# Four network layers on one core: one PSUM pool, Newton steps for the group norm, exponentials put off, and a helper queue with three turns and timed waits

## The chip, the cores and the metric

The kernel runs on one core of a Trainium2 chip. A core has TensorE (matrix products, PE in the profile; its weight loads are PEld), VectorE (DVE), ScalarE (ACT), GpSimd (POOL) and SyncE (SP), and DMA queues. Each engine takes its instructions in the order in which the program gives them, and waits for others by semaphores. PSUM, into which TensorE writes, has eight banks of 128 partitions x 512 fp32 values. The metric is the time of one execution on the device, in microseconds; lower is better.

## The reference, cut to what matters

All values are fp32. Four layers follow each other on `x` of shape (2, 512, 32, 32), which is 2 images of 512 channels by 1024 pixels.

```python
# layer 0: attention with a position bias from a small MLP (unchanged code), then
h1 = gelu(einsum('bchw,oc->bohw', bn(x), mlp_w1) + mlp_b1)          # 512 -> 2048
x  = x + einsum('bchw,oc->bohw', h1, mlp_w2) + mlp_b2               # 2048 -> 512
# layer 1: group norm (32 groups), 8 heads of 64, projection
g  = (g - mean) * rsqrt(var + EPS)
w  = softmax(einsum('bct,bcs->bts', q * s, k * s), axis=-1)         # per head
x  = x + proj(einsum('bts,bcs->bct', w, v))
# layer 2: group norm, one head over all 512 channels
attn = softmax(einsum('bci,bcj->bij', q, k) * C ** -0.5, axis=-1)
x  = x + proj(einsum('bcj,bij->bci', v, attn))
# layer 3: q and k of 64 channels, softmax over the FIRST index
attn = softmax(einsum('bdi,bdj->bij', q, k), axis=1)
x  = gamma * einsum('bci,bij->bcj', v, attn) + x
```

## The kernel before

**Stages.** In the profiled execution layer 0's attention runs to 2043 us and its MLP to 2450. Layer 1 follows: image 0 to about 2645, image 1 to about 2871, the projection of image 0 between. Layer 2 runs for both images to about 3160, layer 3 for both to the end. The program keeps on each engine the order in which it is written. Nothing is reordered, so what is written ahead of an instruction on its engine runs ahead of it.

**A product in seven parts.** Nearly all large products after layer 0 are made by `group`, a scheme that splits both operands in 2x2 blocks and needs seven block products in place of eight. It takes four PSUM banks x, y, v, z and gives TensorE the products in this order: x (the first), y (number 5), v (4), z (3), then more onto x (1), y (6) and v (2). ACT copies x to `p1` after the first product, and v to `p5` after the third (L1408, L1414). DVE makes `u2 = y + p1` (L1411) before product 6 may go onto y, and `u3 = y + p1` (L1420) after it; four outputs are written by `put` (L1434). Products 1 and 6 write over banks that the copy and u2 read first, so TensorE waits if those are late. `nk` is the number of 128-row steps, `n` the columns; the matmul is at L1391. One fp32 matmul instruction leaves two records in the trace.

**Forms.** The scheme needs sums of blocks of each operand: `left_sums` (DVE, L1357 to L1360; tiles `vs` for values) and `right_sums` (L1366 to L1369; tiles `pt` for weights `p`, `ot` for attention outputs), four operations for each small block, called forms below.

**The helper queue.** DVE, ACT and SP work that belongs to later groups is put as items (cost, function) into `tracks`. Each group gives it two turns: `do_chores(slack)` after `p5`, and again after the outputs. A turn runs items track by track until the costs have used up the budget. An `APART` in a track ends that track's turn, which is how a wait for a DMA is spaced. `flush` runs everything that is left in a track, at once, when the next step needs it.

**Softmax sums.** In layers 2 and 3 `Weights` holds the four chunks of p of a half (512 pixels). `acc` adds them on DVE (L1805). `total` sums over partitions with two matmuls against ones into bank `den` (L1819), copies the row and sends it to `few`, 128 partitions wide, by SP DMAs. `divisor` adds the two halves of `few`, inverts and sends the result through DRAM (`d`, L1832) to all partitions (`r`, L1833). In layer 3 (`shares=True`) each chunk of p is multiplied by r (`normalize`, L1837) and formed again before the product `pw3`; in layer 2 the product's output is multiplied (L1872). Attention of layer 1 does alike in `divide`, once per pair of heads and image: `sums`, `invert` (with the DMAs `d`, `r`), `scale` (L1636). Products are named: `pm` heads and projections, `pmv` values, `ppr` layer 1's projection, `score`, `pw` weighted values (`pw2`, `pw3` by layer).

**Group norm.** `group_norm` is a generator whose pieces are items of the queue: BN_STATS for each 128 channels, two small matmuls over groups, then, for the inverse root, `Ln` and `Exp(-0.5 ...)` on ACT and one correction step on DVE (L1103 to L1108).

**Pools.** The MLP has its own PSUM pool with three turning buffers for each of two tiles, and `ps_m` has two banks for the norm. Both close after the MLP; then `banks`, eight turning banks with one tag, opens for all the rest.

Of the kernel before, what the change touches and what calls it, by code (L numbers as in the profile page):

```python
# [19 lines left out]
P = 128  # L20
# [60 lines left out]
def kernel(ctx: ExitStack, tc: tile.TileContext, a: dict, out: bass.AP):  # L81
# [971 lines left out]
    def layers(f, fold_d, t2_b, o2_b):  # L1053
# [19 lines left out]
        def group_norm(x, gname, bname, h, small_psum):  # L1073

            st = small.tile([P, CC, 2, 6], F32, name="st")
            mv = small.tile([P, CC, 2], F32, name="mv")
            for cc in range(CC):
                for half in range(2):
                    nc.vector.bn_stats(st[:, cc, half, :], x[:, cc, half * HALF : (half + 1) * HALF])
                nc.vector.bn_aggr(mv[:, cc, :], st[:, cc].rearrange("p h s -> p (h s)"))  # L1080
                yield

            def over_group(v, name):
                pg = small_psum("pg")[:, :CC]
                nc.tensor.matmul(pg, cs("gmean"), v, start=True, stop=True)
                yield
                g = small.tile([P, CC], F32, name=name)
                nc.vector.tensor_copy(g, pg)  # L1088
                return g

            mean = small.tile([P, CC], F32, name="mean")
            nc.vector.tensor_copy(mean, mv[:, :, 0])
            yield
            gm = yield from over_group(mean, "gm")
            nc.vector.tensor_sub(mean, mean, gm)
            nc.vector.tensor_mul(mean, mean, mean)
            nc.vector.tensor_add(mean, mean, mv[:, :, 1])
            yield
            var = yield from over_group(mean, "var")
            nc.vector.tensor_scalar(var, var, EPS, None, ALU.add)  # L1100

            rs = small.tile([P, CC], F32, name="rs")
            nc.scalar.activation(rs, var, AF.Ln)  # L1103
            nc.scalar.activation(rs, rs, AF.Exp, scale=-0.5)
            nc.vector.tensor_mul(var, var, rs)
            nc.vector.tensor_mul(var, var, rs)
            nc.vector.tensor_scalar(var, var, -0.5, 1.5, ALU.mult, ALU.add)
            nc.vector.tensor_mul(rs, rs, var)  # L1108
            sc = small.tile([P, CC], F32, name="sc")
            sh = small.tile([P, CC], F32, name="sh")  # L1110
            nc.vector.tensor_mul(sc, rs, col(gname, 0, CC))
            nc.vector.tensor_mul(sh, gm, sc)
            nc.vector.tensor_sub(sh, col(bname, 0, CC), sh)
            yield
            normed = chan.tile([P, CC, HW], F32, name="hc")
            h.append(normed)
            for cc in range(CC):
                nc.scalar.activation(
                    normed[:, cc, :], x[:, cc, :], AF.Identity, scale=sc[:, cc : cc + 1], bias=sh[:, cc : cc + 1]
                )  # L1120
                yield

        norm_psum = f.enter_context(ExitStack())
        ps_m = norm_psum.enter_context(tc.tile_pool(name="ps_m", bufs=2, space=PSUM))

        h1s, h2s = [[], []], [[], []]
        norm = group_norm(
            xs[0], "gn_w", "gn_b", h1s[0], lambda name: ps_m.tile([P, HALF], F32, name=name, tag="mm")
        )
# [3 lines left out]
        with ExitStack() as mlp:  # L1133
# [8 lines left out]
            ps = mlp.enter_context(tc.tile_pool(name="mlp_ps", bufs=3, space=PSUM))  # L1142
# [43 lines left out]
            def products(left, right, cols, some, pms=None):  # L1186

                if pms is None:
                    pms = [ps.tile([P, 4, PX], F32, name=f"pm{i}") for i in "ab"]
                a, b = pms  # L1190
                at = {1: a[:, 0], 2: a[:, 1], 6: a[:, 2], 3: a[:, 3], 4: b[:, 0], 5: b[:, 1], 7: b[:, 2]}
                for i in some:
                    product(at[i], i, left, right, cols)
                return pms
# [50 lines left out]
            for c in range(MC):  # L1245
                for m in (MC + c, c):
                    pm = ps.tile([P, BLK], F32, name="pmp", tag="pma")
                    accumulate(pm, [(w1[:, k, m * P : (m + 1) * P], xn[:, k, :]) for k in range(CC)])
                    nc.scalar.activation(hid[:, m, :], pm, AF.Gelu, bias=col("mlp_b1", m))
                form1(nc.vector, slice(c * P, (c + 1) * P))  # L1250
            right1 = normed_rights(1)
            for m in (2, 3, 0, 1):
                pm = ps.tile([P, BLK], F32, name="pmp2", tag="pmb")
                accumulate(pm, [(w2[:, k, m * P : (m + 1) * P], hid[:, k, :]) for k in range(HID // P)])
                added(0, m, pm)
                if m >= 2:
                    form2(nc.vector, slice((m - 2) * P, (m - 1) * P))
# [52 lines left out]
        norm_psum.close()  # L1310
# [3 lines left out]
        banks = f.enter_context(tc.tile_pool(name="banks", bufs=8, space=PSUM))  # L1314

        def bank(name):
            return banks.tile([P, HALF], F32, name=name, tag="bank")

# [9 lines left out]
        tracks = []  # L1328
        APART = None

        def track():
            t = deque()
            tracks.append(t)
            return t

        def do_chores(budget):
            for t in tracks:
                while t and budget > 0:
                    item = t.popleft()
                    if item is APART:  # L1340
                        break
                    cost, f = item
                    f()
                    budget -= cost

        def flush(*some):
            for t in some:
                while t:
                    item = t.popleft()
                    if item is not APART:  # L1350
# [34 lines left out]
        def group(name, nk, n, stationary, moving, evict, slack, plain=False):  # L1385

            x, y, v, z = [bank(name)[:, :n] for _ in range(4)]
# [12 lines left out]
            if plain:  # L1400
# [4 lines left out]
                return  # L1405
            add(x, 0, 0)
# [8 lines left out]
            do_chores(slack)  # L1415
            add(z, 3, 3)
            add(x, 1, 1, False)
            add(y, 6, 6, False)
# [4 lines left out]
            do_chores(slack)  # L1423
# [29 lines left out]
        def statistics(steps, wait):  # L1453
            t = track()
            for i in range(CC + 5):
                t.append((1.5 if i < CC else 0.5, lambda: advance(steps)))
                if i >= CC:
                    t.extend([APART] * wait)
            return t

        def normed(t, steps, h, name):

            for _ in range(CC):
                t.extend(((0.1, lambda: advance(steps)), APART))
# [23 lines left out]
        def project(name, seven_w, seven_h, c, outs, bias, plain=False):  # L1488
# [3 lines left out]
            def evict(c11, c12, c21, c22):  # L1492
# [7 lines left out]
                rows(seven_w, slice(c * P, (c + 1) * P)), lambda i, k: seven_h[i][:, k, :], evict, 4.5, plain,  # L1500
            )

        def values(seven_w, seven_h, s, vt):
# [3 lines left out]
            def evict(c11, c12, c21, c22):  # L1507
# [7 lines left out]
                lambda i, k: seven_h[i][:, k, s * P : (s + 1) * P], lambda i, k: seven_w[i][:, k, :], evict, 2.0,  # L1515
# [34 lines left out]
        def attend(qs, ks, vt):  # L1550

            outs, late, acc = [], None, None
            for i in range(17):
                m, sp = divmod(i, 4)
                ps = {}
                if i < 16:
                    for s in (2 * sp, 2 * sp + 1):
# [9 lines left out]
                        do_chores(0.9)  # L1567
                if late is not None:
# [14 lines left out]
                    if lsp == 3:  # L1583
# [3 lines left out]
                        dividing = divide(o, acc, 3 if i < 16 else 1)  # L1587
# [13 lines left out]
        def divide(o, acc, wait):  # L1601
# [36 lines left out]
            t.extend((APART, (0.1, sums), *[APART] * wait, (0.4, invert), *[APART] * wait, (1.2, scale)))  # L1638
# [18 lines left out]
        def add_projection(x, seven_w, seven_o):  # L1657

            for c in range(2):

                def evict(c11, c12, c21, c22):
# [8 lines left out]
                    "ppr", 2, HALF, rows(seven_w, slice(c * P, (c + 1) * P)), lambda i, k: seven_o[i](k), evict, 2.0  # L1670
# [7 lines left out]
        to_v.extend((APART, APART))  # L1678
# [6 lines left out]
        to_h = statistics(norm, 2)  # L1685
# [48 lines left out]
        to_h = statistics(norm, 2)  # L1734
# [35 lines left out]
        def layer_values(seven_w, seven_h):  # L1770

            vt, unformed, sv, t_s = [], [], [], track()
# [19 lines left out]
        class Weights:  # L1792

            def __init__(self, score, order, at, shares):
                self.score, self.order, self.at, self.shares = score, order, at, shares
                self.p, self.spare, self.track = [], None, track()

            def grow(self, c):
                p = self.score(c)
                self.p.append(p)  # L1800
                if c == 1:
                    self.acc = unit("acc")
                if c:
                    first = self.p[0] if c == 1 else self.acc
                    self.track.append((1.2, lambda: nc.vector.tensor_add(self.acc, first, p)))  # L1805
                if not self.shares:
                    if c == 1:
                        self.form(0)
                    if c:
                        self.form(c)  # L1810
# [3 lines left out]
            def total(self):  # L1814
                acc = self.acc.rearrange(self.order, k=2, q=2)
                den, row = bank("den"), temp("row", HALF)
                self.few = small.tile([P, 2, HALF // P], F32, name="few2")
                for k in range(2):
                    nc.tensor.matmul(den[32 * k : 32 * k + 32], ones[:, :32], acc[:, k], start=True, stop=True)  # L1819
                nc.scalar.copy(row[:64], den[:64])  # L1820
                for k in range(2):
                    nc.sync.dma_start(
                        out=self.few[:, k], in_=row[32 * k : 32 * k + 1].rearrange("o (q n) -> o q n", q=P)
                    )

            def divisor(self):
                few = self.few[:, 0]
                nc.vector.tensor_add(few, few, self.few[:, 1])
# [22 lines left out]
            def finish(self):  # L1851
                self.track.extend((APART, (0.1, self.total), APART, APART, (0.4, self.divisor)))
                if self.shares:
                    self.track.append(APART)
# [4 lines left out]
        def weighed(name, x, qb, seven_sv, w, bias, done=None):  # L1859

            n = slice(qb * HALF, (qb + 1) * HALF)
            for g in range(2):
# [18 lines left out]
                group(name, 4, QUARTER, lambda i, s: seven_sv(i, s)[:, g * P : (g + 1) * P], w.seven, evict, 4.2)  # L1881
                yield

        def scores2(qb, seven_ts, seven_h):

            def score(c):
                p = unit("p2")

                def evict(c11, c12, c21, c22):
# [5 lines left out]
                    nc.scalar.activation(p[:, QUARTER:], p[:, QUARTER:], AF.Exp, scale=C ** -0.5)  # L1895
# [3 lines left out]
                    lambda i, k: seven_ts(i, k, qb), evict, 2.0,  # L1899
# [5 lines left out]
        for b in range(B):  # L1905
# [11 lines left out]
            if b == 0:  # L1917
# [3 lines left out]
                to_h = statistics(norm, 1)  # L1921
# [97 lines left out]
        to_x.append(APART)  # L2019
# [142 lines left out]
```

## Time and profile before

| what | value |
|---|---|
| median of 3 runs (lowest to highest) | 3422.63 us (3417.33 to 3426.73) |
| profiled execution: time, span | 3421.59 us, 3419.8 us |
| mean granted TensorE clock | 0.994 |
| TensorE busy, share of the span | 3364.8 us, 98% |
| DVE, ACT, POOL busy | 78%, 53%, 14% |
| ACT_TABLE_LOAD in the four group norms | 8 x 1.28 us (L1103, L1104) |
| `r<-d` DMAs, issue to landing (median) | 24 of them, 3.5 us |
| last matmul ends, span ends | 3413 us, 3419.8 us |

Each timeline or wait line has engine, source line, operation, and tiles as output<-inputs. A bracket at the end gives the engine's idle time before the instruction and what ended it. `x6` means that six like records are drawn together, so a line's time holds all of them. In the table of stages the columns are busy us and count for each engine, then the granted clock (1.00 is full speed), the busy share of the DMA engines and GB/s.

### The profile page before, as it was taken

The numbers are of one execution on the slowest core, as the hardware profiler recorded it, in microseconds if no ns is written. First come the engines' busy times: TensorE is split into PE (matmuls) and PEld (weight loads), VectorE is DVE, ScalarE is ACT, GpSimd is POOL, SyncE is SP. The second block draws the span as 40 slices with busy tenths as digits, with TensorE's granted clock in tenths as the row PEclk, the third lists the DMA queues.
The fourth block names the chain that finished last, engine by engine and source line by source line (L and its number), as shares of the span: only waits on it lengthen the run. The fifth ranks groups of instructions, "written<-read, shape, count | busy, mean of one in ns | idle before, by whom it ended". The sixth has DMA issues, their size and how long they took to land.

```text
span 3419.8 us, 61213 instructions
## 1 busy us (share of the span) xinstructions
PE 3364.8 (98%) x24837; PEld 1621.9 (47%) x24837; DVE 2660.2 (78%) x3421; ACT 1817.5 (53%) x2781; POOL 463.9 (14%) x563
## 2 busy tenths in 40 slices
PE   9999999999999999999999999999999999999997
PEld 4333333333333333333333339999753534678776
DVE  6999999999997999999999954555456375646555
ACT  4866867867865767867767631112136163212220
POOL 0222222222221222222222210000000000000000
PEclk9999999999999999999999999999999999999998
DMA  5676676666665576676776740000101010000010
GB/s 168 148 151 138 139 155 142 146 145 139 148 145 110 121 152 142 144 148 139 150 149 134 148 134 24 14 14 11 47 0 32 7 35 20 4 4 19 13 38 29
DMA packets 145555, 320.30 MB, mean 94 GB/s; under 512 B 29936, under 2 KB 75632, under 8 KB 144496
## 3 DMA queue, kind: packets, MB, share of 16 engines
q0 software_dynamic: 56880, 199.79, 30.7%
q1 hardware_dynamic: 87088, 111.78, 10.7%
q8 instruction: 198, 3.24, 0.4%
q10 hardware_dynamic: 1296, 4.72, 0.4%
q14 instruction: 93, 0.76, 0.1%
HBM read 71.46 MB, written 10.83 MB: 24 GB/s over the span
## 4 chain that ended last, share of the span: by engine, by line
PE 74%; DVE 18%; issue 5%; ACT 2%; DMA 1%; SPq 0%; POOL 0%; DVEq 0%; ACTq 0%; POOLq 0%
PE z L543 33%; DVE wa L526 7%; PE pw L1391 5%; PE pma L136 5%; DVE h L557 5%; PE pmb L136 4%; PE pmv L1391 3%; PE score L1564 3%; PE pv L1576 3%; PE score L1391 3%; DVE h L526 2%; PE pm L1391 2%; PE pmp L136 2%; PE pp L629 1%; PE ppr L1391 1%
## 5 line engine op out<-in xcount | busy, mean ns | idle before, releaser
L543 PE MATMUL z<-wa,cpb_w 128*32 128x512 f32 x11904 | 1779.1, 593 | 6.7 <-DVE simbias L490 3.4
L552 ACT ACTIVATE h<-z,b2h 128x1024 f32<-128x1024 f32 x1024 | 1134.8, 1114 | 529.0 <-PE z L543 505.6
L543 PE MATMUL z<-h,cpb_w 128*32 128x512 f32 x4480 | 986.3, 593 | 3.3 <-ACT h L552 2.2
L543 PEld LDWEIGHTS z<-wa,cpb_w 128*32 128x32 f32 x11904 | 493.0, 110 | 883.7 <-issue 804.8
L526 DVE CUSTOM_DVE_ANT_1 wa<-tab,tab 128x1024 f32<-128x1024 f32 x744 | 881.3, 1224 | 33.9 <-PE z L543 33.8
L557 DVE SCALAR_TENSOR_TENSOR h<-h,turn,h 128x1024 f32<-128x1024 f32 x512 | 657.1, 1283 | 8.8 <-ACT h L552 8.5
L543 PEld LDWEIGHTS z<-h,cpb_w 128*32 128x32 f32 x4480 | 256.3, 110 | 335.0 <-issue 291.7
L832 POOL DMA_DIRECT2D h<-h x255 | 226.9, 890 | 1064.3 <-DVE h L557 712.9
L526 DVE CUSTOM_DVE_ANT_1 h<-tab,tab 128x1024 f32<-128x1024 f32 x280 | 334.3, 1224 | 10.5 <-PE z L543 10.4
L1213 ACT COPY p<-pma 128x128 f32<-128x128 f32 x70 | 18.6, 265 | 301.4 <-PE pma L136 301.4
L1565 ACT ACTIVATE p<-score 128x512 f32<-128x512 f32 x256 | 130.0, 624 | 74.9 <-PE score L1564 73.9
L1205 DVE TENSOR_TENSOR upper<-pma,p 128x256 f32<-128x256 f32 x70 | 29.6, 422 | 163.4 <-ACT p L1213 163.3
L825 POOL DMA_DIRECT2D h<-h x126 | 109.8, 872 | 331.3 <-DMA h<-h 327.9
L829 POOL DMA_DIRECT2D h<-h x126 | 120.0, 952 | 137.2 <-DMA h<-h 131.9
L1597 DVE TENSOR_TENSOR acc<-acc,p 128x1024 f32<-128x1024 f32 x96 | 110.9, 1219 | 17.7 <-ACT p L1565 17.7
L1564 PE MATMUL score<-q,k 64*128 64x512 f32 x512 | 120.2, 603 | 1.1 <-DVE gm L1088 1.1
L1576 PE MATMUL pv<-p,vT 128*64 128x512 f32 x512 | 116.5, 598 | 0.0
L1391 PE MATMUL pw<-p,vT 128*128 128x256 f32 x384 | 92.4, 389 | 10.3 <-DVE p L1837 10.2
L513 ACT ACTIVATE tab<-tab,pc 128x512 f32<-128x512 f32 x126 | 96.2, 763 | 0.0
L1391 PE MATMUL pmv<-wa,hc 128*128 128x256 f32 x384 | 90.9, 384 | 2.9 <-DVE u L1420 2.1
L1391 PEld LDWEIGHTS pw<-p,vT 128*128 128x128 f32 x384 | 72.8, 193 | 27.7 <-DVE p L1837 13.6
L347 ACT ACTIVATE products<-qpad,pc 128x64 f32<-128x64 f32 x252 | 85.5, 407 | 0.0
(437 smaller groups left out, 3708.0 us busy)
## 6 DMA issues: line engine op xcount, KB each, us to landing
h<-h POOLq DMA_DIRECT2D x255, 512.0 KB, 4.9
h<-h POOLq DMA_DIRECT2D x252, 256.0 KB, 4.9
tab<-slog_d SPq DMA_DIRECT2D x128, 256.0 KB, 4.5
h<-h SPq DMA_DIRECT2D x126, 256.0 KB, 2.3
r<-d SPq DMA_DIRECT2D x24, 256.0 KB, 3.5
xt<-in_xt SPq DMA_DIRECT2D x8, 512.0 KB, 7.9
wa<-in_mlp_w SPq DMA_DIRECT2D x4, 1024.0 KB, 8.0
wb<-in_mlp_w SPq DMA_DIRECT2D x16, 256.0 KB, 5.7
```

The lines of the kernel that those rows point to most:

```text
L136: nc.tensor.matmul(pm, w, m, start=(k == 0), stop=(k == len(pairs) - 1))
L526: nc.vector._custom_dve(TENSOR_ADD_SAT, out=h1.rearrange("p (y x) -> p y x", x=W), in0=tx[:, quad, point, :].unsqueeze(1).to_broadcast([P, ...
L543: nc.tensor.matmul(z[point * 32 : point * 32 + 32, n], cpb_w2[:, lo : lo + 32], h1s[point][:, n], start=True, stop=True,)
L552: nc.scalar.activation(h2, z, AF.Relu, bias=b2h[:, part : part + 1])
L557: nc.vector.scalar_tensor_tensor(h2, h2, turn[:, part // 2 : part // 2 + 1], parts.pop(part + 1), ALU.mult, ALU.add)
L829: nc.gpsimd.dma_start(out=joins[i - 3][1:P:2], in_=joins.pop(i - 2)[1:P:2], accum_op=ALU.add)
L832: nc.gpsimd.dma_start(out=joins[i - 1], in_=other, accum_op=ALU.add)
L1391: nc.tensor.matmul(out, stationary(l, k), moving(r, k), start=start and k == 0, stop=k == nk - 1, skip_group_check=not start,)
L1564: nc.tensor.matmul(sc, ks[m][r, s * P : (s + 1) * P], qs[m][r, n], start=True, stop=True)
L1565: nc.scalar.activation(p[:, part], sc, AF.Exp, scale=64 ** -0.5)
L1576: nc.tensor.matmul(pv[half][part * 64 : part * 64 + 64], vt[s % 4][:, lo : lo + 64], lps[s, half][:, part, :], start=(s == 0), stop=(s == 7),)
L1597: nc.vector.tensor_add(acc[half], acc[half], ps[s, half])
```

## The change

- **One pool.** `ps_m` and the MLP's pool are gone. `banks` (eight banks) opens ahead of the first norm and serves the MLP's tiles too.
- **Inverse root.** `Ln`, `Exp` and the correction become an integer first guess from the bits of the variance and four Newton steps, thirteen DVE operations on 128x4 values.
- **Queue.** A track holds plain numbers as waits, in us by the queue's own clock. Each turn advances that clock by a nominal time (`nk*n/256` in a group, 3.4 in attention), and a track is passed over until its wait is up. Each group has three turns: after `p5`, after products 3 and 1, and at the end. Budgets are smaller (4.5, 4.2 and 2.0 become 2.6, 2.6 and 1.1). Waits are set at each place in place of APART. The track of the value sums of layers 2 and 3 goes first.
- **Put off.** Layer 2's exponential over 768 columns runs in the next group, after its `p5` copy; so does what belongs to the fourth chunk of p (forms, sum, hops).
- **Weights.** In layer 3 two sums, p0+p1 and p2+p3, replace the running one (two DVE additions in place of three). `total` then has four matmuls and four DMAs to `few`, and `divisor` three additions of 128x4.

```diff
-            nc.scalar.activation(rs, var, AF.Ln)
-            nc.scalar.activation(rs, rs, AF.Exp, scale=-0.5)
-            nc.vector.tensor_mul(var, var, rs)
-            nc.vector.tensor_mul(var, var, rs)
-            nc.vector.tensor_scalar(var, var, -0.5, 1.5, ALU.mult, ALU.add)
-            nc.vector.tensor_mul(rs, rs, var)
+            square = small.tile([P, CC], F32, name="square")
+            nc.vector.tensor_scalar(
+                rs.bitcast(mybir.dt.int32), var.bitcast(mybir.dt.int32), -0.5, float(0x5F3759DF), ALU.mult, ALU.add
+            )
+            for _ in range(4):
+                nc.vector.tensor_mul(square, rs, rs)
+                nc.vector.scalar_tensor_tensor(square, square, -0.5, var, ALU.mult, ALU.mult)
+                nc.vector.scalar_tensor_tensor(rs, square, 1.5, rs, ALU.add, ALU.mult)
...
-        norm_psum = f.enter_context(ExitStack())
-        ps_m = norm_psum.enter_context(tc.tile_pool(name="ps_m", bufs=2, space=PSUM))
+        banks = f.enter_context(tc.tile_pool(name="banks", bufs=8, space=PSUM))
...
-            ps = mlp.enter_context(tc.tile_pool(name="mlp_ps", bufs=3, space=PSUM))
...
-                    pms = [ps.tile([P, 4, PX], F32, name=f"pm{i}") for i in "ab"]
+                    pms = [bank(f"pm{i}").rearrange("p (j n) -> p j n", j=4) for i in "ab"]
...
+        def do_chores(us, budget):
+            clock[0] += us
             for t in tracks:
-                while t and budget > 0:
+                while t and budget > 0 and t.ready <= clock[0]:
                     item = t.popleft()
-                    if item is APART:
-                        break
-                    cost, f = item
-                    f()
-                    budget -= cost
+                    if isinstance(item, float):
+                        t.ready = clock[0] + item
+                    else:
+                        cost, f = item
+                        f()
+                        budget -= cost
...
         def group(name, nk, n, stationary, moving, evict, slack, plain=False):
+            third = nk * n / 256
...
             nc.scalar.copy(p5, v)
-            do_chores(slack)
+            at_once(later)
+            do_chores(third, slack)
             add(z, 3, 3)
             add(x, 1, 1, False)
+            do_chores(third, slack)
             add(y, 6, 6, False)
...
             evict((x, None), (v, u2), (z, u3), (p5, u3))
-            do_chores(slack)
+            do_chores(third, slack)
...
-                        do_chores(0.9)
+                        do_chores(3.4, 0.9)
...
-            t.extend((APART, (0.1, sums), *[APART] * wait, (0.4, invert), *[APART] * wait, (1.2, scale)))
+            t.extend((2.0, (0.1, sums), 5.0, (0.4, invert), 6.5, (1.2, scale)))
...
-            vt, unformed, sv, t_s = [], [], [], track()
+            vt, unformed, sv, t_s = [], [], [], track(True)
...
-                if c == 1:
-                    self.acc = unit("acc")
-                if c:
-                    first = self.p[0] if c == 1 else self.acc
-                    self.track.append((1.2, lambda: nc.vector.tensor_add(self.acc, first, p)))
...
+                if self.shares:
+                    self.grown(c)
+                else:
+                    if c:
+                        self.grown(c - 1)
+                    if c == 3:
+                        put_off.append(lambda: self.grown(3))
...
+                if c % 2 and self.shares or c == 1:
+                    self.acc.append(unit("acc"))
+                    self.add(self.acc[-1], p[c - 1], p[c])
+                elif c > 1 and not self.shares:
+                    self.add(self.acc[0], self.acc[0], p[c])
...
-                self.track.extend((APART, (0.1, self.total), APART, APART, (0.4, self.divisor)))
+                self.track.extend((2.0, (0.1, self.total), 4.0, (0.4, self.divisor)))
                 if self.shares:
-                    self.track.append(APART)
+                    self.track.append(5.0)
...
-                    nc.scalar.activation(p[:, QUARTER:], p[:, QUARTER:], AF.Exp, scale=C ** -0.5)
+                    put_off.append(
+                        lambda: nc.scalar.activation(p[:, QUARTER:], p[:, QUARTER:], AF.Exp, scale=C ** -0.5)
+                    )
```

## The prediction

> **What bounds the kernel now.** I read the page first: busy times, then the slices.
>
> ```profile
> span 3419.8 us, 61213 instructions
> PE 3364.8 (98%) x24837; PEld 1621.9 (47%) x24837; DVE 2660.2 (78%) x3421; ACT 1817.5 (53%) x2781; POOL 463.9 (14%) x563
> ...
> PEclk9999999999999999999999999999999999999998
> ```
>
> TensorE computes for 98% of the span, and the change alters no product of it but four small den matmuls. So only what TensorE does not compute, or computes slowly, can be won. The stages say where that is; the change begins at the MLP, at 2043 us.
>
> ```profile
> core 0: us, PE busy (x) PEld busy (x) DVE busy (x) ACT busy (x) POOL busy (x), PEclk, DMA share, GB/s
> 2043.00:2450.00 407.00, 407.00 (x3394) 399.43 (x3395) 203.61 (x625) 81.52 (x207) 17.80 (x31) 1.00 0.09 29
> 2450.00:2645.00 195.00, 192.97 (x762) 85.33 (x763) 112.70 (x150) 91.14 (x172) 0.00 (x0) 0.99 0.04 11
> ...
> 3160.00:3420.00 260.00, 236.41 (x1018) 180.16 (x1018) 143.30 (x292) 47.88 (x104) 0.00 (x0) 0.95 0.10 27
> ```
>
> The MLP has no idle TensorE time, so three turning PSUM buffers more or fewer win nothing there. The last stage has the most, at clock 0.95. The waits of TensorE after 2000 us name the sites:
>
> ```profile
> engine line waited for: us in total, times, longest us
> PE pw L1391 <- DVE p L1837: 10.2, 5, 3.2
> PE pw L1391 <- DVE vs L1358: 5.6, 7, 1.0
> PE score L1391 <- ACT p L1408: 2.9, 1, 2.9
> PE pmv L1391 <- DVE u L1420: 2.1, 1, 2.1
> PE pm L1391 <- issue: 2.0, 1, 2.0
> ```
>
> All of these are DVE or ACT work that stands ahead of what TensorE needs, save the last. A wait costs more than itself: matmuls behind a long one run slow. From TensorE's timeline:
>
> ```profile
> 2452.47 4.51 PE L1391 MATMUL pm<-hc,wa 128*128 128x512 f32 x6 [2.03 <-issue]
> 2966.02 3.78 PE L1391 MATMUL score<-t,hc 128*128 128x256 f32 x8 [2.90 <-ACT p L1408]
> 3351.08 4.10 PE L1391 MATMUL pw<-pt,vs 128*128 128x256 f32 x10 [0.96 <-DVE vs L1358]
> ```
>
> Elsewhere a record of 512 columns takes 0.43 us and one of 256 columns 0.2145. The first line's six should take 2.6 and took 4.5: the gap of 2.03 cost 3.9 in all. The second line's gap of 2.90 cost 6.2 with what follows it. I measured every late start of a matmul this way (start to start, less the pitch). After 2449 us they sum to 45 us; that is all that can be won.
>
> **Part by part.** Each term is this execution's stall and what I leave of it after walking the new order of DVE, ACT and the chores past it.
>
> *One pool.* The stall at 2452 is a pool that opens only when the old ones are free: TensorE waits for no data (its releaser is "issue"), while the last combined adds of the MLP end at 2453.0. With eight turning banks, the first group takes banks released long before; the forms it reads are done at 2460, five microseconds before their use. -3.9 (none stays; at worst 1.0, were the first bank one of the last add's).
>
> *Newton steps.* Two table loads stand in the chain of the norm that lies among layer 2's scores:
>
> ```profile
> 2956.70 1.28 ACT L1103 ACT_TABLE_LOAD   x1
> 2957.99 0.21 ACT L1103 ACTIVATE rs<-var 128x4 f32<-128x4 f32 x1
> 2958.22 1.28 ACT L1104 ACT_TABLE_LOAD   x1
> ...
> 2959.75 0.16 DVE L1105 TENSOR_TENSOR var<-var,rs 128x4 f32<-128x4 f32 x1 [3.55 <-ACT rs L1104]
> ```
>
> DVE stands still 3.55 us. Thirteen small operations replace four, nine more at a pitch of 0.2: +1.8, so DVE runs 1.75 earlier. The put-off exponential then clears ACT: the 768-column one took 0.84 ahead of the copy of p1 that TensorE waited for, and itself waited for DVE's sums. Without both, the copy is in time, and u2 (done 2966.7, now 2964.9) meets a need at 2964.0 to 2964.9: 0 to 1.0 stays, I take 0.6. -5.6. The other three norms lie in attention or projections where DVE's idle time cost TensorE nothing, so their six loads (7.7 us of ACT) and 5.4 us of added DVE are worth zero.
> The Trainium skill speaks here ("ScalarE: Activation LUTs", What ACT_TABLE_LOAD costs): a load of 1283 ns, and a drain of some 1380 ns besides. The row has the first figure, but the Ln starts 10 ns after its load; by the page two drains, 2.8 us, would be won on top, by the row none.
>
> *Queue: three turns, sums of values first, smaller budgets.* Forms of 0.42 (0.34 to 0.46 apart), sums of 0.69 and pixels' adds of 1.22 move among turns.
> - 2686 and 2945: u2 behind eight flushed sums, or two BN_STATS (1.28): with fewer ahead, -0.8 and -1.0. At 2907 one more 0.68 lands ahead: +0.65.
> - 3006 and 3155, each 1.4: last value sums, flushed just ahead of pw. One fewer: 0.95 stays, -0.9 for both. At 3253 den's 1.05 us of matmuls covered the sums and is moved away: 0.39 becomes 0.95, +0.55.
> - 3346 to 3352: sixteen sums flushed after the last values, 5.9 by four waits. Put first in the queue, twelve go beside the values: 0.95 stays, -4.95.
> - 3307: den waits 0.67 for a chain of three acc; two independent pairs, timed 2.0 later: -0.65.
>
> *Normalising in layer 3.* Block of one normalise (1.22) and four forms: 2.85 us on DVE, pw3 needs all four.
> - 3286: three were flushed; the 4.0 goes if the three turns of value and score groups take them, which their hops allow. -4.0 (at worst 0).
> - 3227: DVE now blocks 4.62 us on r, with u3 behind. In the new order the den and its four row transfers (two more on SP, 0.58 each) start in layer 2's last pw2 groups. r lands about 3212.7, 7 us ahead, so DVE no longer blocks; but the first normalise and its forms come in front of u2 of the first pmv, 2.2 to 3.2 us, with 1.7 of slow clock: 4.9 against 4.0. +0.9 (from -4 to +2).
> - 3378 to 3388: four blocks, no TensorE work between, 13.1. One block fits the second group of the pw3 before, three stay flushed: 3 x 2.85 + 1.7 = 10.3. -2.8 (from 0, were none to fit, to -8.5, were all).
>
> Both leftovers carry a slow clock of 1.7, from the row at 2452. The Trainium skill ("TensorE: Matmul & The Clock Gate", Part 1) puts the clock at half only after an idle window of about 3.4 us; here gaps of 2.03 had it, and 0.96 (the 3351 line) had not. By the page these two terms would be 3.4 smaller, by the rows not.
>
> *What is hidden.* Put-off grown(3) and the two-add acc: 1.2 us of DVE less per layer-3 block, where DVE is 55% busy. In attention a scale now comes two turns of 3.4 after its invert. Its r takes 9.2 (2669.8 to 2679.0 in the trace), so DVE waits about 2.4 with its acc adds behind. Already now DVE waits 14.7 us in five such places (up to 3.7), and TensorE not once. Zero; the second rival prices it.
>
> Sum: -3.9 -5.6 -0.8 -1.0 +0.65 -0.9 +0.55 -4.95 -0.65 -4.0 +0.9 -2.8 = -22.5. The profiled execution took 3421.6; 3399 by it. The median of the runs is 1.0 higher: 3400.
>
> **Rivals.** *Half of it comes back* (3412): smaller budgets leave more for the flushes, and DVE, a little behind at each, meets u2 late. For it: DVE's blocks of 2.85 us can only stand before something. Against: it is 55 to 61% busy there. Price: 3286 and 3378 stay (+6.8) and 3227 takes its bad end (+1.1), some 4 late u2 of 1 us each: +12.
>
> *Slower* (3433): in attention DVE's wait for r counts. Eight divides x 2.4 = 19 us of late acc and bank copies, each with 1.7 of slow clock, 14: 33 on 3400. It decides once DVE falls over about 8 us behind, the lag that acc bears now without a wait of TensorE. The five free waits in the trace speak against it.
>
> *Nearly all goes* (3385): 3378 by 8.5 rather than 2.8, 3227 by 4.0 rather than +0.9, 2907 and 3253 stay where they are, and the three leftovers of 0.95 go: 5.7 + 4.9 + 1.2 + 2.9 = 15 more.
>
> **How the numbers follow.** My forecast (3393 to 3407) 0.55, half back 0.22, nearly all 0.13, slower 0.10. The range 3384 to 3416 leaves out the slower case and the far tail of half back. 0.3% is 10.3 us, about what a measurement of this kernel can tell from no change: faster lies below 3412.4. Forecast and nearly all are there whole, 0.68; half back for some half, 0.11. Same takes the rest of half back and a little of the slower case, 0.13; slower 0.08.
>
> **What would show it.** Right: no gap at the first pm after the MLP; no ACT_TABLE_LOAD at L1103; the score wait on L1408 gone; vs waits below 3.5 us in total; the p L1837 wait still there, last and longest, some 6 to 8 us. Wrong: a wait of TensorE for acc or o in attention; more than 3 us on u lines among the pmv of layer 3; a span above 3410.

## The result, and the profile after

| | before | changed |
|---|---|---|
| median of 5 runs (lowest to highest) | 3425.15 us (3417.33 to 3426.73) | 3404.29 us (3400.25 to 3404.69) |
| ratio, 95% interval | | 0.9941 (0.9927 to 0.9956) |
| profiled execution: time, span | 3421.59, 3419.8 us | 3400.25, 3398.4 us |
| mean granted clock | 0.994 | 0.997 |

The changed kernel is faster by 0.59%: 20 us, between 15 and 25. The forecast was 3400 within 3384 to 3416. First the same parts of the page, after:

```profile
span 3398.4 us, 61331 instructions
PE 3351.9 (99%) x24853; PEld 1615.5 (48%) x24853; DVE 2662.6 (78%) x3461; ACT 1803.4 (53%) x2764; POOL 464.0 (14%) x563
```

TensorE does the same products and, in four blocks of layer 3, two den matmuls more (8 matmuls, 16 records; the prediction named only four), and yet it is busy for 13 us less. Busy time includes slow matmuls, so part of the gain is speed and not waiting. The waits of TensorE after 2400 us (line waited for: us in total, times, longest):

```profile
PE pw L1392 <- DVE p L1853: 6.9, 3, 3.1
PE pmv L1392 <- DVE u L1413: 5.2, 3, 3.7
PE pw L1392 <- DVE vs L1357: 3.5, 4, 0.9
PE score L1568 <- DVE gm L1088: 1.1, 1, 1.1
PE score L1392 <- DVE u L1413: 0.7, 1, 0.7
```

"Issue" and the score's wait on L1408 (now L1410) are gone, vs went from 5.6 to 3.5, p from 10.2 to 6.9. Before, the waits after 2400 us that the view lists came to 26.6 us; these are 17.4. That is 9.2 of 21. The late starts measured as in the prediction (start to start, less the pitch) went from 44.9 to 24.4 us, 20.5 less, so the other 11 us are matmuls that no longer run slow behind a wait, and starts too little late for the view. (Both sums hold 1.3 us at a score that waits for `gm`, the same in both kernels, which the table leaves out.)

By site, in us, each from its own trace (a0 and a1 are the program's names for the first and second half of image 0 in layer 3, and a block is the normalise and the four forms of one chunk of p):

| site in before's trace | before | forecast left | changed |
|---|---|---|---|
| 2452, first pm after the MLP | 3.9 | 0 | 0 |
| 2686 and 2945, u2 | 1.8 | 0 | 0 |
| 2907, u2 of pmv | 0.9 | 1.55 | 1.8 (1.43 and a new 0.41) |
| 2966, score | 6.2 | 0.6 | 0.85 |
| 3006, 3155, 3253, vs | 3.2 | 2.85 | 3.1 |
| 3227, first pmv of layer 3 | 4.0 | 4.9 | 5.6 |
| 3286 and 3307, a1's blocks, den | 4.7 | 0 | 0 |
| 3346, vs of the last half | 5.9 | 0.95 | 1.04 |
| 3378, last normalise blocks | 13.1 | 10.3 | 10.6 |

The gap after the MLP is closed, and the score's wait is now one of u2. From TensorE's timeline:

```profile
2448.23 1.95 PE L136 MATMUL pma<-hid,w2s 128*128 128x128 f32 x16
2450.01 8.32 PE L1392 MATMUL pm<-hc,wa 128*128 128x512 f32 x19
...
2965.73 1.13 PE L1392 MATMUL score<-t,hc 128*128 128x256 f32 x4 [0.68 <-DVE u L1413]
```

Nineteen records of 0.43 are 8.2 us: no gap and full speed.

### The profile page after: what moved, and what is told of

Same layout as the page of the kernel before. It is cut to its first block, busy times and chain, and to the rows that moved or that the text cites. A ratio compares the mean times of both kernels' runs of the same rounds, so it can differ in the third digit from the quotient of the medians.

```text
span 3398.4 us, 61331 instructions
## 1 busy us (share of the span) xinstructions
PE 3351.9 (99%) x24853; PEld 1615.5 (48%) x24853; DVE 2662.6 (78%) x3461; ACT 1803.4 (53%) x2764; POOL 464.0 (14%) x563
## 4 chain that ended last, share of the span: by engine, by line
PE 77%; DVE 16%; issue 4%; ACT 2%; DMA 1%; ACTq 0%; POOL 0%; DVEq 0%; SPq 0%; POOLq 0%
PE z L543 35%; DVE wa L526 6%; PE pma L136 5%; PE pw L1392 5%; PE pmb L136 4%; DVE h L557 4%; PE pmv L1392 4%; PE score L1568 3%; PE pv L1580 3%; PE pm L1392 3%; PE score L1392 3%; DVE h L526 2%; PE pmp L136 2%; PE pp L629 2%; PE ppr L1392 1%
## 5 line engine op out<-in xcount | busy, mean ns | idle before, releaser
L526 DVE CUSTOM_DVE_ANT_1 h<-tab,tab 128x1024 f32<-128x1024 f32 x280 | 332.9, 1216 | 10.5 <-PE z L543 10.4
```

The source lines that it names most:

```text
L526: nc.vector._custom_dve(TENSOR_ADD_SAT, out=h1.rearrange("p (y x) -> p y x", x=W), in0=tx[:, quad, point, :].unsqueeze(1).to_broadcast([P, ...
```

## The experiments

Ratios are to runs of the kernel before on the same chip; numbers at a site come from the run's one profiled execution, and the span is that execution's. The changed kernel's ratio is 0.9941.

**One part alone, on the kernel before.**

```diff
-        norm_psum = f.enter_context(ExitStack())
-        ps_m = norm_psum.enter_context(tc.tile_pool(name="ps_m", bufs=2, space=PSUM))
+        banks = f.enter_context(tc.tile_pool(name="banks", bufs=8, space=PSUM))
...
-            ps = mlp.enter_context(tc.tile_pool(name="mlp_ps", bufs=3, space=PSUM))
```

> The kernel before with the one pool of eight banks alone. Theory (each stall is a cost by itself, and goes with the edit that lies at its site): the late start of the first pm after the MLP, 3.9 us with its slow clock, goes and every other wait stays; 3.9 us less, 3419. Rival (parts lean on each other): with the first heads 4 us earlier the forms of layer 1 or its statistics come late instead, a new wait on vs or u lines before 2560 us, and the time stays within 1 us.

0.9996 (0.9987 to 1.0005). The first pm's late start is gone, but the time did not follow clearly: a slow stretch that cost 3.4 us came at 2655 us, behind products that nothing in the edit touches (see the last section). No late vs or forms of layer 1: the rival's wait did not come.

```diff
-            nc.scalar.activation(rs, var, AF.Ln)
-            nc.scalar.activation(rs, rs, AF.Exp, scale=-0.5)
...
+            for _ in range(4):
+                nc.vector.tensor_mul(square, rs, rs)
...
```

> The kernel before with the Newton steps alone. Theory: DVE's 3.55 us of idle time in layer 2's scores becomes 1.8 us of work, so the score wait on L1408 (2.90 us, 6.2 with slow clock) shrinks by 1.75 to about 1.15, which is too short for a slow clock: 4 to 5 us less, and the other three norms give nothing. Rival (the exponential ahead of the copy is the cause): the wait stays over 2 us and the gain is under 2 us.

0.9996 (0.9987 to 1.0005), but at its site the theory held. The wait on the copy fell from 2.9 us, with no slow clock behind it:

```profile
PE score L1393 <- ACT p L1410: 1.1, 1, 1.1
```

The late start went from 6.2 to 1.3, 4.9 less; the other three norms gave nothing. The time does not show it clearly: its interval runs from 4.4 us less to 1.7 more.

```diff
-                    nc.scalar.activation(p[:, QUARTER:], p[:, QUARTER:], AF.Exp, scale=C ** -0.5)
+                    put_off.append(lambda: nc.scalar.activation(p[:, QUARTER:], p[:, QUARTER:], AF.Exp, scale=C ** -0.5))
```

> The kernel before with the put-off alone: layer 2's 768-column exponential and what belongs to the fourth chunk, in its old queue of two turns. Theory: the copy of p1 is no longer behind the exponential, but DVE still idles 3.55 us for the two table loads, so u2 comes at about 2966.7 against a need at 2964: the wait on L1408 turns into a wait on the u line of some 2.3 us with a slow clock behind; 1 to 2.5 us less. Rival (the exponential is the cause): the whole wait goes, 5.6 us less.

1.0002 (0.9993 to 1.0011). As expected the wait changed its name: u2 in place of the copy, 3.1 us. The late start fell to 3.3, as no slow clock followed in this profile, but the time did not fall by the 1 to 2.5 us expected. The wait did not go, so the exponential was no cause by itself.

Both of these edits together:

> The kernel before with Newton steps and put-off, no other part. Theory: the stall at 2966 falls from 6.2 to under 1.0, as in the changed kernel, 5.2 to 5.6 us less, 3416 to 3417; the stalls of layer 3 stay as before. Rival (the queue's three turns are needed for it): more than 2 us stay.

0.9991 (0.9982 to 1.0). 0.73 and 0.17 are left of 6.2: 5.3 less at the site, without the third turn. So at the site Newton does 4.9 of it, put-off the small rest, and alone put-off moves the wait. The time is some 3 us less, with an interval that reaches no change.

**One part undone, in the changed kernel.**

```diff
-            vt, unformed, sv, t_s = [], [], [], track(True)
+            vt, unformed, sv, t_s = [], [], [], track()
```

> The changed kernel, but the track of the value sums of layers 2 and 3 stands in its old place instead of first. Theory: the first of the sixteen vs operations of layer 3's last half are left for the flush again, and the four waits of about 1 us at the start of its pw3 come back for 1.0: 4 to 5 us more than the changed kernel, about 15 us less than before. Rival (the third turn alone gives them room): under 1.5 us more.

0.9930 (0.9918 to 0.9942): not slower at all. The first theory fell; the rival's bound (under 1.5 us more) holds, but not its reason. The vs waits did come back, 5.1 us in place of 3.5 (3.7 of late starts at the last half), but the last normalise blocks, 10.6 us, vanished:

```profile
PE pmv L1392 <- DVE u L1413: 5.7, 3, 3.5
PE pw L1392 <- DVE vs L1357: 5.1, 6, 1.0
PE score L1568 <- DVE gm L1088: 1.1, 1, 1.1
PE score L1392 <- DVE u L1413: 0.7, 1, 0.7
```

There is no line for p. The sums of values, put first, use up the budgets of the turns, and the last half's acc waits behind them. In the changed kernel acc of p2 and p3 ran at 3334.8; its divisor and first normalise were these:

```profile
3346.64 0.18 DVE L1845 RECIPROCAL few<-few 128x4 f32<-128x4 f32 x1
...
3352.66 1.23 DVE L1853 TENSOR_TENSOR p<-p,r 128x1024 f32<-128x1024 f32 x1 [4.51 <-DMA r<-d]
```

With the sums last, acc ran at 3324.3, and DVE did not wait for r:

```profile
3334.21 0.18 DVE L1845 RECIPROCAL few<-few 128x4 f32<-128x4 f32 x1
...
3341.77 1.22 DVE L1853 TENSOR_TENSOR p<-p,r 128x1024 f32<-128x1024 f32 x1
```

What the prediction took for room in the turns is the time at which r lands. The reverse was tried too, the sums first in the kernel before, with nothing else:

> The kernel before, with the track of the value sums put first and nothing else changed. Theory (each stall is its own): the four vs waits of layer 3's last half shrink to one, 4.5 to 5 us less than before. Rival (sums put first delay the last half's acc, and with it r and the normalise blocks): the stall of the last flush, 13.1 in before, already has all four blocks behind it and grows by the time that r is later, 2 to 4 us; the net gain is under 2.5 us.

1.0042 (1.0029 to 1.0056), 14 us slower. The rival named the mechanism, and priced it too low:

```profile
PE pw L1391 <- DVE p L1837: 25.4, 8, 9.5
...
3388.72 0.18 DVE L1829 RECIPROCAL few<-few 128x4 f32<-128x4 f32 x1
3394.89 1.23 DVE L1837 TENSOR_TENSOR p<-p,r 128x1024 f32<-128x1024 f32 x1 [5.73 <-DMA r<-d]
```

The wait on normalise grew from 10.2 to 25.4. The vs waits of the last half fell as they should (5.9 to 1.75 of late starts), but the divisor came after the last outputs, and DVE stood 5.7 us for r with all four blocks behind it (late starts 13.1 to 19.4); a1's blocks went the same way (4.0 to 16.4). In the changed kernel, then, the other parts of the queue must first make up for this.

```diff
-            third = nk * n / 256
+            half = nk * n / 256 * 1.5
...
             add(x, 1, 1, False)
-            do_chores(third, slack)
             add(y, 6, 6, False)
...
```

> The changed kernel with two turns in each group and the old budgets (4.5, 4.2, 2.0), the clock of the queue advanced by half a group at each; waits in us, sums first, put-off, Newton and pool stay. Theory: what is won by the order and the hops stays (first pm, score, vs), but larger turns put more ahead of u2, and the normalise blocks crowd: late u lines grow by 1 to 2 us each at some three places and the stall at a1's normalise (4 us before) comes back in part; 3 to 8 us more than the changed kernel. Rival (turns do not matter, only order and waits): within 2 us of the changed kernel.

0.9950 (0.9938 to 0.9962), about 3 us more, with intervals that overlap, and 4.4 in the span, of which 3.3 is the slow stretch at 2655 us again. So the total does not tell the two expectations apart. At the sites it is a trade: a1's blocks are flushed again (9.7 us of late starts, where the changed kernel has none) and one u2 is 2.2 late, but the last blocks come to 2.4 in place of 10.6 and the first pmv to 0.4 in place of 5.6.

```diff
-                if c % 2 and self.shares or c == 1:
+                if c == 1:
...
-                elif c > 1 and not self.shares:
+                elif c > 1:
```

> The changed kernel with one running sum in layer 3 again: three additions of 1.22 in place of two, and den with two matmuls and two DMAs in place of four. Theory: 1.2 us of DVE more in each of four blocks, and den 1 us later behind the third addition: 0 to 3 us more, most of it in the normalise blocks of the last half (one fewer fits ahead of the flush would be 2.9 more). Rival (four row DMAs at 0.58 each are what makes r late, DVE blocked 5.2 us on it at 3197): the block shortens by over 1 us, and the time falls by 1 to 3 us.

0.9963 (0.9950 to 0.9977), some 7 us more, 5.1 in the span, which is over what either expected. Late starts of 5.5 at a1's blocks come back. The rival has a part of the truth too, in the first pmv: 2.3 in place of 5.6. Its divisor stands one turn later there, and its first block goes behind the outputs instead of holding them up.

**r sooner.** The two stalls left should fall if den comes a turn earlier.

```diff
-                self.track.extend((2.0, (0.1, self.total), 4.0, (0.4, self.divisor)))
+                self.track.extend((0.0 if self.shares else 2.0, (0.1, self.total), 4.0, (0.4, self.divisor)))
```

> The changed kernel with the wait of 2.0 ahead of the den matmuls at 0 in layer 3, so that den, row DMAs and divisor come a turn sooner. Theory (the two stalls left in layer 3, 5.6 and 10.6 us with slow clock, are set by when r lands): in the last half r lands some 4 us sooner, the first normalise moves up to the first turn of the second pw3 group and two more blocks fit before the flush, 10.6 becomes 3 to 5; at 3197 DVE blocks a turn earlier with less behind it, 5.6 becomes 1 to 4. 7 to 11 us less than the changed kernel, 3393 to 3397. Rival (DVE's order, not r, sets it: what moves up only pushes u2 and the outputs back): within 2 us, with new waits on u lines.

0.9918 (0.9904 to 0.9932), 3392.48 us: 8 us less than the changed kernel, as expected. The last blocks' late start is 2.0, the first pmv's 2.3:

```profile
PE pmv L1392 <- DVE u L1413: 4.5, 4, 2.2
PE pw L1392 <- DVE vs L1357: 3.5, 4, 0.9
PE pw L1392 <- DVE p L1853: 1.9, 1, 1.9
```

DVE's idle time on r after 3160 us fell from 11.1 us to 1.0.

Den sooner, and the value sums last:

> The kernel with den a turn sooner, and the value sums' track in its old place. Theory (the two orders serve the same end, and only one is needed): with den sooner the last half's blocks already fit, so what the old place does is only to bring back the vs waits, 3.7 us in place of 1.0, against 2.0 us that is still left at the last flush: within 2 us of den sooner alone. Rival (both gains add): 2 us or more less than den sooner alone.

0.9922 (0.9909 to 0.9936). With den sooner the two orders cannot be told apart (3395.48 against 3392.48 us, on different chips), and no stall of the last blocks is left: both serve the same end.

```diff
-            do_chores(third, slack)
+            do_chores(third, slack if end is None else end)
...
-                group(name, 4, QUARTER, lambda i, s: seven_sv(i, s)[:, g * P : (g + 1) * P], w.seven, evict, 2.6)
+                group(name, 4, QUARTER, lambda i, s: seven_sv(i, s)[:, g * P : (g + 1) * P], w.seven, evict, 2.6,
+                      end=None if w.shares else 0.0)
```

> The kernel with den a turn sooner, and besides nothing is taken from the queue in the last turn of a pw2 group. Theory: the u2 of the first pmv of layer 3 is 2.33 us late because a normalise block stands ahead of it in the turn that ends the group; the block moves behind u2 and this wait goes: 2 us less than with den sooner alone, no new wait over 1 us. Rival (the block is late wherever it stands): it comes back at a later u2, or ahead of pw3, and the time stays within 1 us or rises.

0.9914 (0.9900 to 0.9927), 3391.73 us. The late u2 of layer 3's first pmv went from 2.33 to under 0.13, but 1.05 came at a1's blocks, as the rival said: at best 1 us, which the times do not show. By the ratios this is the fastest version run, 0.27% below the changed kernel, but its interval overlaps those of the other two with den sooner.

**DVE's waits in attention.**

```diff
-            t.extend((2.0, (0.1, sums), 5.0, (0.4, invert), 6.5, (1.2, scale)))
+            t.extend((2.0, (0.1, sums), 5.0, (0.4, invert), 3.0, (1.2, scale)))
```

> The changed kernel with the wait of 6.5 ahead of attention's scale at 3.0, so that DVE stands at the scale one turn sooner and waits some 3 us longer for r in each of the divides. Theory (DVE's waits in attention are free, the lag of acc bears them): TensorE waits for no acc and no o in attention, and the time is within 2 us of the changed kernel, while DVE's idle time on r grows from 17.8 us by 10 or more. Rival (the slower case of the prediction, these waits count): new waits of TensorE on acc or o lines between 2550 and 2870 us, 8 to 20 us more.

0.9966 (0.9954 to 0.9978), 8.5 us more. DVE's idle time at the first seven of the eight scales (us, times), in the changed kernel and then here:

```profile
  DMA r<-d: 17.8, 5
```

```profile
  DMA r<-d: 44.7, 7
```

TensorE waits for acc or o in neither, and from its first score to its last attention takes 111.8 us for image 0 and 114.0 for image 1 in both. So within attention these waits are free, as the theory says. But the last scale of each image stands among projections, ahead of a u2 (DVE waits 8.9 us there for image 0, which is in the row, and 10.4 for image 1, which is the eighth), and there the wait is paid:

```profile
PE pmv L1392 <- DVE u L1413: 8.0, 3, 3.7
PE pm L1392 <- DVE u L1413: 2.9, 1, 2.9
```

Late starts are 3.0 at 2687 us (none in the changed kernel) and 3.2 at 2906 (0.4). That is 5.9 of the 8.4 us in the span; the slow stretch at 2655 us adds 3.4, and the last blocks are 0.8 less late. The theory was right for attention; the rival was right that such waits can count, but they came on u2, not on acc or o.

## Why the prediction was right, point by point

*The total.* Forecast -22.5; the sites gave -20.5, the span -21.4, the runs -20.2 by the ratio. The working by sites held: eleven of the twelve terms are within 0.4 us of the measured change. Newton with put-off: -5.6 forecast, -5.3 measured; the u2 at 2907: +0.65 and +0.9; the last blocks: -2.8 and -2.5.

*The first pmv of layer 3: the size was near (+0.9, measured +1.7), the step was wrong.* The prediction said that r lands 7 us ahead and DVE no longer blocks. From the changed kernel, DVE and then TensorE:

```profile
3202.00 1.22 DVE L1853 TENSOR_TENSOR p<-p,r 128x1024 f32<-128x1024 f32 x1 [5.21 <-DMA r<-d]
...
3209.09 1.22 DVE L1853 TENSOR_TENSOR p<-p,r 128x1024 f32<-128x1024 f32 x1
...
3211.94 0.42 DVE L1413 TENSOR_TENSOR u<-pmv,p 128x256 f32<-128x256 f32 x1
```

```profile
3212.41 1.13 PE L1392 MATMUL pmv<-wa,hc 128*128 128x256 f32 x4 [3.71 <-DVE u L1413]
```

DVE blocks longer than before (4.62), on a normalise that stands ahead of u3. The outputs of that group, a second block and only then u2 follow. The wait of 5.0 is two turns by the queue's clock, but DVE reaches the normalise as soon as it has nothing ahead of it: the queue sets an order, not a time. The prediction gave "more than 3 us on u lines among the pmv of layer 3" as a sign that it is wrong, and 3.7 is there; this step was. Den sooner takes it to 2.3, and the end turn left free to nothing.

*The sums first: the term was right (-4.95, measured -4.9), and the price was left out.* It was costed at nothing elsewhere; alone it costs 14 us net, and in the change most of the 10.6 us at the last blocks. The prediction explained those by room in the turns ("one block fits"). One block did go ahead of the flush, but what set this was that r came late: with r sooner, in the kernels with the sums last and with den sooner, the 10.6 fell to nothing and to 2.0. That this term agreed was luck.

*The slow rival.* DVE's waits in attention were free in the changed kernel, 17.8 us of them. Its condition, a lag of over 8 us behind acc, no run put to the test. What cost time with the scale early was another thing: the two places where a scale stands ahead of u2. The 0.41 us that is new at 2907 in the changed kernel is one of them.

*The clock.* The prediction read from two rows that a gap of 2.03 brings a slow clock and one of 0.96 none. The second is a misreading: the ten records at 3351 took 4.10 us, where ten such records behind one gap in the changed kernel took 2.43:

```profile
3333.63 2.43 PE L1392 MATMUL pw<-pt,vs 128*128 128x256 f32 x10 [0.88 <-DVE vs L1357]
```

So 1.7 of the 5.9 us at this site were slow clock. The sum does not change, since the whole 5.9 was counted. Ahead of the 0.96 at 3351 stand three more gaps of 0.7 to 0.9. The four kernels with pool, Newton, put-off or the last two together have a like row of four gaps, and were slow behind it; the kernel with the sums last was slow behind gaps of 0.79 and 0.96. A gap of 0.96 by itself (3007 in before) was followed by full speed.

A long gap does not always bring it either. The same 2.03 gap after the MLP, in the kernel with put-off alone, and its gap of 3.09:

```profile
2453.79 4.53 PE L1391 MATMUL pm<-hc,wa 128*128 128x512 f32 x10 [2.03 <-issue]
...
2970.43 1.13 PE L1391 MATMUL score<-t,hc 128*128 128x256 f32 x4 [3.09 <-DVE u L1412]
```

Ten records of 0.43 are 4.3 us: full speed. Of the five kernels with the gap after the MLP, four were slow behind it (3.8 to 3.9 us in all) and this one was not (2.2). So the 1.7 us in the two leftovers were a likely value, not a rule. The Trainium skill ("TensorE: Matmul & The Clock Gate", Part 1) has the clock's window running freely, so that the point of transition varies from run to run. The five profiles fit that, though no run here shows the window. They do not fit its length, about 3.4 us, as a least gap: slow matmuls that cost 1.7 us followed gaps of 2.03.

What stays open: why one part alone (pool, Newton, put-off) moved the median by less than its site. The intervals reach some 3 us either way, and the slow stretch at 2655 us came in some kernels' profiles and not in others; no run held it fixed, and every number at a site is from one execution. The clock alone moves as much: of the 33 runs of the kernel before on that chip, the five with a mean granted clock of 0.996 took 3417.2 us on average, and the seven with 0.993 took 3424.2.

## What to carry to other kernels

Where one engine is 98% busy, list its late starts by site, walk the helper engine's order at each, and sum: here the sum of twelve terms came within 2 us. A queue that orders work by priority moves what is not first: before putting something ahead, find the longest chain (here sum, row DMAs, inverse, broadcast, normalise, forms) that it delays, since here putting plain additions ahead of a chain through DMAs won 4 us and lost 19 at the sites. A wait for a DMA on an in-order engine is free only if nothing urgent stands behind it.

## What the runs showed of the hardware that was not expected

Four den matmuls, each into 32 partitions of its own, take the time of two: one line of TensorE's timeline before, and one of the changed kernel.

```profile
3355.11 1.05 PE L1819 MATMUL den<-acc,ones 128*32 128x512 f32 x4
```

```profile
3339.44 1.06 PE L1834 MATMUL den<-acc,ones 128*32 128x512 f32 x8
```

And the clock can drop without any gap in TensorE's work: a stretch of 32 bias products of one column ran at full speed in the changed kernel. In the kernel with Newton and put-off its last nine came 0.21 us apart rather than 0.11, and the four records of 512 columns behind it took 3.76 us rather than 1.96.

```profile
2648.68 3.63 PE L136 MATMUL pb<-vb,proj 128*128 128x1 f32 x32
...
2652.17 1.96 PE L1392 MATMUL pm<-h1t,wa 128*128 128x512 f32 x4
```

```profile
2652.99 4.55 PE L136 MATMUL pb<-vb,proj 128*128 128x1 f32 x32
2657.40 3.76 PE L1393 MATMUL pm<-h1t,wa 128*128 128x512 f32 x4
```

TensorE counts as busy in both. From the first of these products to the 65th record, both kernels and three experiments took 15.1 us, two (sums last, den sooner) 16.8 and the other seven 18.4: 1.7 and 3.4 us of slow clock in nine of the twelve experiments' profiles, which no edit accounts for. What sets it is not shown.
